# Turning the adjacency by VectorE and DRAM instead of by TensorE in the first graph stage

## The chip, the cores and the metric

The kernel runs on one core of one Trainium2 chip. The metric is the device time of one execution in microseconds (us); the number compared is the median over runs. The engines are named as the profile names them: PE is TensorE's matmul and PEld its weight load, DVE is VectorE, ACT is ScalarE, POOL is GpSimd and SP is SyncE. SPq and POOLq mark copies (DMAs) that SP and Pool put into their queues.

## The reference

There are 16 batches of 1024 nodes with 256 channels, and one adjacency `adj` of 1024 x 1024, all float32. Two layers follow each other:

```python
# layer 0: graph attention
h = relu(layernorm(x))
c = mean over channels of h                      # one value for each node
A = abs(abs(sigmoid(c_j - c_i) - 0.5) - 0.5) * 2
g = relu((h^T @ (adj * (A + A^T) / 2)) * para)   # becomes the queries
k, v = split(h @ kv_w)                           # 4 heads of 64
x = x + softmax(q k^T * scale) v
# layer 1: normalized adjacency and two linear layers
h = relu(layernorm(x))
A1 = adj + I
deg = colsum(A1) + rowsum(A1) - diag(A1)
A_hat = A1 * rsqrt(deg)[:, None] * rsqrt(deg)[None, :]
x = x + batchnorm(relu(batchnorm((A_hat @ h) @ W1^T + b1)) @ W2^T + b2)
```

Layer 0 needs `adj` as it lies in memory, weighted anew for each batch. Layer 1 needs `A_hat` transposed in SBUF (tile `f_ahatT`), because the contraction has to lie on the partitions. `f_ahatT` is made once, in the first batch's stages, and is used for the first time after the second batch's graph stage.

## The kernel before

The program is one instruction stream for each engine, in the order in which the code is written (`tc.manual_schedule`): no scheduler moves anything, and waits are by semaphores on the tiles. An engine that waits holds up everything that is queued behind the waiting instruction. SP and Pool issue copies in the same way, and each copy of a queue also waits for the landing of the one eight places before it in that queue.

For each batch b the stages are `graph(b)`, `attention(b)` and, one batch behind, layer 1's `linear1_all`. Batch 0 is prepared by a prologue. The partition count is P = 128, there are NC = 8 chunks of 128 nodes, and CC = 2 halves of the channels.

**Prologue.** SP loads x of batch 0, the eight adjacency tiles `f_adj`, `f_kvw`, x of batch 1 and `f_w1n`. The layer norm leaves `f_h_a` and the sums `f_sums`. `prepare_row(0)` turns the sums into rows with 16 small transposes on TensorE (L317 into `first`, L323 into `second`), VectorE copies `second` into `f_row` (L333), ScalarE makes the first weights `f_w` and VectorE masks them with `adj` (L336).

**graph(0).** For each chunk c a list of hooks runs, and then TensorE multiplies `f_h_a` with the weights `f_w` of chunk c into two PSUM tiles `f_gps` (L489, eight matmuls of 512 columns a chunk, four in each of the two halves' tiles). `weights(0, c)` is two ScalarE operations (L350, L353) and one VectorE mask (L367). `turn_h` transposes h in blocks (f_hQ, L378) and distributes the blocks by 16 copies on SP and 16 on Pool into `f_hT` (L385). At c = 5 SP issues the loads of `f_para` (L482). After the chunks VectorE multiplies `f_gps` with `f_para` into `f_qT` (L518), and the keys K and values V are made from `f_hT` by seven products each (class `Seven`; L428 and L433 on TensorE, L443 copies on ScalarE, L446 additions on VectorE). Their PSUM tiles come from a pool of three (`fps_s`, tag "s"), two of which `f_gps` holds until L518 has read them; `K.product(1)` takes the first that L518 frees, at 50.14 us.

**The turn of the adjacency.** Spread over the prologue and the hooks of chunks 1 to 5, `turn_adj(i)` and `turn_adj_aside(i)` transpose tile i in eight TensorE instructions (L1372; L1387 in two PSUM banks of other pools) and `place_adj` copies the result from PSUM to `f_ahatT` (L1378, L1393; seven tiles by VectorE, one by ScalarE). The view `columns(i)` orders the columns so that nodes of one residue modulo 8 stand together.

**After graph(0).** `diagonal()` runs on Pool: for each of eight blocks it multiplies the block with the identity into a spare tile (L1412) and adds the identity to it (L1413); VectorE reduces the products to `f_diag` (L1414). `column_sums(m)` are ScalarE copies with a running sum (L1404), two at the end of each of attention(0)'s four quarters; `roots` makes `f_dinv` from the sums after the last, and `scale_adj` applies it in graph(1) (L1433). Attention's quarters are 32 matmuls of scores (`f_s`, L868), ScalarE's exponentials (`f_p`, L876), VectorE's additions (L882, L888, L891, L896) and 32 matmuls with the values (`f_o`, L920). In the third quarter VectorE also inverts the softmax sums (`f_rec`, L953 and on) and ScalarE spreads them (`f_recs`, L962) ahead of the next quarter's exponentials.

Three small loads and stores come up in the prediction besides: `fw1T` and `fw2T` are the turned weights of the two linear layers on their way to DRAM (L1455, on Pool), `f_w2n` is the load of W2 in four copies of 32 partitions each (L1442, on SP), and `fw1s` and `f_att` are later copies on SP (L1158, L988).

Of the kernel before, what the change touches and what calls it, by code (L numbers as in the profile page):

```python
# [10 lines left out]
F32 = mybir.dt.float32  # L11
AF = mybir.ActivationFunctionType
ALU = mybir.AluOpType
AX = mybir.AxisListType
# [15 lines left out]
def fast_path(  # L30
# [37 lines left out]
    gs_d = [dram.tile([P, 4 * NC // 2, P], F32, tag=f"fgs_{b}", name=f"fgs_{b}") for b in range(B)]  # L68
    w1T_d = dram.tile([P, CC, F1], F32, tag="fw1T", name="fw1T")
    w2T_d = dram.tile([P, FC, C], F32, tag="fw2T", name="fw2T")  # L70
    w1s_d = dram.tile([P, 4, FC * P // 2], F32, tag="fw1s", name="fw1s")
    kvs_d = dram.tile([P, 8, P], F32, tag="fkvs", name="fkvs")
    t_d = [dram.tile([P, 4, 512], F32, tag=f"ft_{k}", name=f"ft_{k}") for k in range(3)]
# [104 lines left out]
    with ExitStack() as stage:  # L178
# [212 lines left out]
        class Seven:  # L391
# [50 lines left out]
            def copy(self, i, j):  # L442
                nc.scalar.copy(self.c(i, j), self.ps["x"])  # L443
# [26 lines left out]
        def graph(b, between):  # L470
# [42 lines left out]
            if b == 0:  # L513
                V, K = projections(b, kT, v, part, kt, key_sums[0])
                V.product(1)
                V.copy(0, 0)
                for d in range(CC):
                    nc.vector.tensor_mul(qT[:, d, :], gps[d], para_t[d])  # L518
                V.product(2)
                V.add(0, 0, 2)  # L520
                K.product(1)
                K.copy(0, 0)
                V.product(6)
                V.copy(1, 0)
                V.product(7)
                K.product(2)
                K.add(0, 0, 2)
                V.product(5)
                V.copy(1, 1)
                V.add(1, 0, 7)  # L530
                V.add(1, 1, 7)
                K.product(6)
                K.copy(1, 0)
                V.product(4)
                V.add(1, 0, 4)
                V.product(3)
                V.copy(0, 1)
                K.product(5)
                K.copy(1, 1)
                K.product(7)  # L540
                K.add(1, 0, 7)
                K.add(1, 1, 7)
                K.product(4)
                K.add(1, 0, 4)
                for d in range(CC):
                    nc.scalar.activation(qT[:, d, :], qT[:, d, :], AF.Relu, scale=-SCALE)
                K.product(3)
                K.copy(0, 1)
                return qT, kT, v
# [806 lines left out]
        def columns(i):  # L1356

            view = ahatT.rearrange("p m (i q) -> p m i q", i=NC)
            return view[:, :, :, ROW * i : ROW * (i + 1)]
# [6 lines left out]
        dinv = small.tile([P, NC], F32, tag="dinv", name="f_dinv", bufs=1)  # L1366
        drow = []

        def turn_adj(i):
            ps = ps_s.tile([P, NC, P], F32, tag="s", name=f"f_adjps_{i}")  # L1370
            for m in range(NC):
                nc.tensor.transpose(ps[:, m, :], adj_t[i][:, ts(m, P)], ident)  # L1372
            turned_adj[i] = ps

        turned_adj = {}

        def place_adj(i, copy):
            copy(columns(i), turned_adj.pop(i).rearrange("p m (q i) -> p m i q", i=NC))  # L1378

        def turn_adj_aside(i):  # L1380

            turned_adj[i] = [
                ps_o.tile([P, NC // 2, P], F32, tag="o", name=f"f_adjpsa_{i}"),
                ps_t.tile([P, NC // 2, P], F32, tag="t", name=f"f_adjpsb_{i}"),
            ]
            for m in range(NC):
                nc.tensor.transpose(  # L1387
                    turned_adj[i][m // 4][:, m % 4, :], adj_t[i][:, ts(m, P)], ident
                )

        def place_adj_aside(i, copy):
            for n, ps in enumerate(turned_adj.pop(i)):
                copy(columns(i)[:, 4 * n : 4 * n + 4], ps.rearrange("p m (q i) -> p m i q", i=NC))  # L1393

        def unused(name):
            return pp.tile([P, N], F32, tag="p", name=f"f_unused_{name}")
# [11 lines left out]
        def diagonal():  # L1408
            on = unused("d").rearrange("p (m q) -> p m q", q=P)
            for m in range(NC):  # L1410
                block = columns(m)[:, m]
                nc.gpsimd.tensor_mul(as_columns(on[:, m, :]), block, as_columns(ident))  # L1412
                nc.gpsimd.tensor_add(block, block, as_columns(ident))  # L1413
            nc.vector.tensor_reduce(diag, on, AX.X, ALU.add)  # L1414

        def roots():
            nc.vector.tensor_add(deg, rsum, deg)
# [41 lines left out]
        with tc.manual_schedule(engines={ENG.PE, ENG.Activation, ENG.DVE, ENG.Pool, ENG.SP}):  # L1459
# [13 lines left out]
            norm.relu(HALF, BY_VECTOR, False)  # L1473
            norm.vector_scale(BY_VECTOR, NC)
            hs[0] = norm.h
            turn_adj(0)
            place_adj(0, nc.vector.tensor_copy)
            xs[1] = load_x(1)
            prepare_row(0)
            turn_adj(1)  # L1480
            turn_adj_aside(2)
            place_adj(1, nc.vector.tensor_copy)
            weights(0, 1)

            w1n = load_rows(W1, FC, "w1")
# [2 lines left out]
            def load_w1T():  # L1488
# [3 lines left out]
                0,  # L1492
                {
                    0: [lambda: weights(0, 2), lambda: turn_h(0)],
                    1: [
                        lambda: place_adj_aside(2, nc.vector.tensor_copy),
                        lambda: weights(0, 3),
                        lambda: turn_adj(3),
                        lambda: place_adj(3, nc.scalar.copy),
                    ],  # L1500
                    2: [
                        lambda: weights(0, 4),
                        lambda: turn_weights(w1n, unused("w1Q"), w1T_d, FC),
                        lambda: prepare_start(1),
                        lambda: turn_adj_aside(4),
                        lambda: place_adj_aside(4, nc.vector.tensor_copy),
                    ],
                    3: [
                        lambda: weights(0, 5),
                        lambda: turn_adj(5),  # L1510
                        lambda: place_adj(5, nc.vector.tensor_copy),
                    ],
                    4: [
                        lambda: weights(0, 6),
                        lambda: weights(0, 7),
                        lambda: turn_adj_aside(6),
                        lambda: place_adj_aside(6, nc.vector.tensor_copy),
                        *(lambda m=m: row_sums(m) for m in range(NC)),
                    ],
                    5: [  # L1520
                        lambda: turn_adj(7),
                        lambda: place_adj(7, nc.vector.tensor_copy),
                    ],
                    6: [
                        lambda: prepare_end(1),
                        make_key_sums,
                        load_w1T,
                        lambda: again(0),
                    ],
                    8: [lambda: prepare_row(1)],  # L1530
                },
            )
            w2n = load_rows(W2, CC, "w2")
            w2Q, w1s_t = (w4.tile([P, N], F32, tag="w4", name=f"f_{n}") for n in ("w2Q", "w1s"))
            diagonal()
            for b in range(B):

                hooks, aside, behind = {}, {}, None
                if b + 1 < B:
# [8 lines left out]
                        behind = lambda: masked(b + 1, 1)  # L1548
                    if b == 0:
                        for m in range(NC):  # L1550
                            hooks.setdefault(m // 2, []).append(lambda m=m: column_sums(m))
                        hooks[1].append(lambda: turn_weights(w2n, w2Q, w2T_d, CC))
                        hooks[2].append(make_w1_sums)
                        hooks[3].append(roots)
# [978 lines left out]
```

## Time and profile before

| what | value |
|---|---|
| median of 3 runs | 2361.14 us (2360.05 to 2361.91) |
| profiled execution, its own time | 2359.81 us |
| its span in the profile | 2358.0 us |
| busy: PE, DVE, ACT, POOL | 2318.3, 1994.6, 1416.5, 447.6 us |
| first matmul of the first graph stage (L489) | 15.86 us |
| its last chunk over, first product for K and V (L433) | 48.35 us |
| first scores of attention(0) (L868) | 60.71 us |
| first chunk of graph(1) (L489) | 117.05 us |

Times within the execution are microseconds from the start of the span. A line of the timeline has the start, the length, the engine, the line of the code, the operation, output and input tiles, the shape and the number of instructions that were merged into the line; a bracket tells how long the engine sat idle before it and what ended that. The profile comes from one execution, so its durations are added up against that execution's own time.

### The profile page before, as it was taken

To read this page: it belongs to the slowest core of one execution; us is meant where nothing else is said; L and a number is where in the kernel's file an instruction comes from. 1 tells how busy PE (TensorE), PEld (TensorE's weight loads), DVE (VectorE), ACT (ScalarE), POOL (GpSimd) and SP (SyncE) were. 2 spreads that over 40 slices of the span, in tenths; PEclk is the share of its full clock that TensorE was granted. 3 is DMA by queue.
4 is the path that set the end of the run, shared out by engine and by line. 5 is a ranking of instruction groups with operands and counts; after the bars stand their busy time and mean duration, and the time that the engine had idled before them with its cause. 6 is when DMAs were issued, how large, how long until landed. Compare 5 with 4: busy or idle time off the path is not lost.

```text
span 2358.0 us, 25776 instructions
## 1 busy us (share of the span) xinstructions
PE 2318.3 (98%) x8256; PEld 1029.6 (44%) x8256; DVE 1994.6 (85%) x2937; ACT 1416.5 (60%) x2057; POOL 447.6 (19%) x573
## 2 busy tenths in 40 slices
PE   8999999999999999999999999999999999999995
PEld 5353444434343434444343434343444434444444
DVE  7988989898979899897989798988989898757766
ACT  6846556574838465655657384746556575346644
POOL 5121212122221112221212221221212121100000
PEclk9999999999999999999999999999999999999998
DMA  6143443423342434335343324252343421355569
GB/s 205 46 143 99 140 137 117 161 107 120 135 137 69 173 91 165 112 134 143 113 134 137 116 88 155 88 179 99 134 143 116 155 77 54 130 214 175 170 241 382
DMA packets 169217, 326.42 MB, mean 138 GB/s; under 512 B 34928, under 2 KB 102000, under 8 KB 169072
## 3 DMA queue, kind: packets, MB, share of 16 engines
q1 hardware_dynamic: 145264, 268.02, 33.3%
q0 software_dynamic: 19200, 39.88, 6.3%
q10 hardware_dynamic: 4608, 16.78, 1.8%
q8 instruction: 67, 1.10, 0.2%
q14 instruction: 78, 0.64, 0.1%
HBM read 203.96 MB, written 101.77 MB: 130 GB/s over the span
## 4 chain that ended last, share of the span: by engine, by line
PE 96%; DMA 1%; DVE 1%; ACT 1%; issue 0%; SPq 0%; DVEq 0%; ACTq 0%; POOLq 0%; POOL 0%
PE f_s L868 19%; PE f_o L920 19%; PE f_aps L1085 16%; PE f_gps L686 8%; PE f_zps L1195 7%; PE f_gpsx L686 6%; PE f_zx L1755 4%; PE f_zm L1755 3%; PE f_vpsx L433 2%; PE f_kpsx L428 2%; PE f_gps L489 2%; PE f_vps L433 2%; PE f_kps L428 2%; PE f_outps L1973 1%; PE f_zps L1278 1%; PE f_zps3b L1195 1%
## 5 line engine op out<-in xcount | busy, mean ns | idle before, releaser
L876 ACT ACTIVATE f_p<-f_s 128x1024 f32<-128x1024 f32 x512 | 476.9, 1045 | 59.5 <-PE f_s L868 59.5
L868 PE MATMUL f_s<-f_qT,f_kT 64*128 64x512 f32 x2048 | 456.8, 596 | 0.0
L920 PE MATMUL f_o<-f_p,f_v 128*64 128x512 f32 x2048 | 453.6, 595 | 0.0
L868 PEld LDWEIGHTS f_s<-f_qT,f_kT 64*128 64x128 f32 x2048 | 191.2, 185 | 263.7 <-issue 118.0
L920 PEld LDWEIGHTS f_o<-f_p,f_v 128*64 128x64 f32 x2048 | 141.4, 137 | 304.3 <-issue 264.2
L363 POOL TENSOR_TENSOR f_w<-f_w,f_adj 128x1024 f32<-128x1024 f32 x56 | 132.2, 2361 | 701.3 <-ACT f_w L362 528.7
L988 POOL DMA_DIRECT2D f_att<-f_oT x256 | 136.1, 539 | 342.9 <-DVE f_oT L971 337.3
L891 DVE TENSOR_TENSOR f_acc<-f_acc,f_p 128x1024 f32<-128x1024 f32 x128 | 155.9, 1218 | 4.6 <-ACT f_p L876 4.6
L891 DVE TENSOR_TENSOR f_sums<-f_sums,f_p 128x1024 f32<-128x1024 f32 x128 | 155.8, 1218 | 0.0
L350 ACT ACTIVATE f_w<-f_row,f_col 128x1024 f32<-128x1024 f32 x127 | 147.4, 1160 | 13.8 <-DMA f_row<-frow 11.5
L353 ACT ACTIVATE f_w<-f_w 128x1024 f32<-128x1024 f32 x127 | 134.3, 1058 | 4.0
L1085 PE MATMUL f_aps<-f_ahatT,f_hs 128*128 128x512 f32 x256 | 115.1, 592 | 0.0
L1085 PE MATMUL f_aps<-f_ahatT,f_h_b 128*128 128x512 f32 x256 | 112.6, 592 | 0.0
L1085 PE MATMUL f_aps<-f_t,f_hs 128*128 128x512 f32 x256 | 112.5, 592 | 0.0
L362 ACT ACTIVATE f_w<-f_w,f_now 128x1024 f32<-128x1024 f32 x56 | 64.3, 1149 | 76.0 <-DVE f_now L360 76.0
L686 PE MATMUL f_gps<-f_w,f_h_a 128*128 128x512 f32 x224 | 109.8, 592 | 0.0
L882 DVE TENSOR_TENSOR f_acc<-f_p,f_p 128x1024 f32<-128x1024 f32 x64 | 77.9, 1217 | 25.0 <-ACT f_p L876 25.0
L888 DVE TENSOR_TENSOR f_sums<-f_p,f_p 128x1024 f32<-128x1024 f32 x64 | 78.1, 1221 | 20.2 <-ACT f_p L876 20.1
L367 DVE SCALAR_TENSOR_TENSOR f_w<-f_w,f_adj 128x1024 f32<-128x1024 f32 x71 | 87.9, 1257 | 7.8 <-ACT f_w L353 7.7
L283 ACT ACTIVATE f_h_a<-f_x,f_shift_a,f_rstd_a 128x256 f32<-128x256 f32 x126 | 73.8, 587 | 31.9 <-DVE f_shift_a L268 31.8
L1218 ACT ACTIVATE f_z<-f_zps,f_b 128x512 f32<-128x512 f32 x60 | 38.0, 684 | 75.2 <-PE f_zps L1195 75.2
L283 ACT ACTIVATE f_h_b<-f_x,f_shift_b,f_rstd_b 128x256 f32<-128x256 f32 x128 | 66.2, 592 | 25.8 <-DVE f_shift_b L268 25.8
(297 smaller groups left out, 3981.9 us busy)
## 6 DMA issues: line engine op xcount, KB each, us to landing
f_t<-ft SPq DMA_DIRECT2D x84, 512.0 KB, 9.7
fz<-f_z SPq DMA_DIRECT2D x64, 512.0 KB, 9.7
f_x<-in_x_dram SPq DMA_DIRECT2D x31, 1024.0 KB, 6.1
f_zb<-fz SPq DMA_DIRECT2D x42, 512.0 KB, 4.5
fx<-f_x SPq DMA_DIRECT2D x16, 1024.0 KB, 4.4
fgs<-f_gs POOLq DMA_DIRECT2D x28, 512.0 KB, 3.0
fhT<-f_hQ POOLq DMA_DIRECT2D x112, 128.0 KB, 3.2
f_hT<-fhT SPq DMA_DIRECT2D x28, 512.0 KB, 6.4
```

Source lines behind the costliest of these rows:

```text
L283: nc.scalar.activation(self.h[:, c, :], self.xt[:, c, :], AF.Relu, bias=self.shift[:, c : c + 1], scale=self.rstd[:, c : c + 1], accum_out ...
L350: nc.scalar.activation(w, rows[b], AF.Abs, bias=cols[b][:, c : c + 1], scale=0.5 / C)
L353: nc.scalar.activation(w, w, AF.Tanh)
L686: nc.tensor.matmul(ps, left, right, start=fresh and n == 0, stop=(n == PAIRS - 1), skip_group_check=more,)
L868: nc.tensor.matmul(ps[:, e, :], kT[rows_e, pair, ts(m, P)], qT[rows_e, pair, ts(g, 512)], start=True, stop=True,)
L876: nc.scalar.activation(p, ps, AF.Exp)
L891: nc.vector.tensor_add(to, to, p)
L920: nc.tensor.matmul(o_of[s][e * HD : (e + 1) * HD, :], v[:, m, ts(2 * pair + e, HD)], p[:, e, :], start=(m == 0), stop=(m == NC - 1),)
L988: queue.dma_start(t[ts(j, 32), :, a].rearrange("r h c i -> r h (c i)"), oT[ts(a, 32), :, j].rearrange("r h c i -> r h (c i)"),)
L1085: nc.tensor.matmul(ps, left[:, m, :], right(m), start=not more and m == 0, stop=(m == KH - 1), skip_group_check=more,)
L1195: nc.tensor.matmul(ps[i], left[:, ts(i, P)], right, start=not more, stop=True, skip_group_check=more,)
L1755: nc.tensor.matmul(ps, left[:, m, :], right[:, m, :], start=start and m == 0, stop=(m == 1), skip_group_check=not start,)
```

## The change

The turn of `adj` leaves TensorE. The adjacency is loaded a second time with its rows in another order (`by_rows`: node number 8u + i, so that 32 partitions hold rows u of one residue i), VectorE transposes it in blocks of 32 x 32 into `f_ahatT`, which serves as a staging area (`stage_rows`), Pool stores the blocks to a DRAM tile `fadjT` so that they land where the transposed matrix wants them, and SP loads the whole of it back into `f_ahatT`. Each of these copies is written for 32 partitions at a time; the stores go in runs of 128 elements. Half of the rows is loaded before the first graph stage (on Pool's queue, into the still unused tiles `kT` and `qT`), the other half on SP behind the `f_hT` copies. Four turns run in the hooks of chunks 1 to 3, four among the K and V products ("first" and "then"); `prepare_row(1)` moves to "first". VectorE's reduction for the diagonal moves from the place before attention(0) to the end of the third quarter, and the column sums from two in every quarter to none, two, three and three.

```diff
+    adjT_d = dram.tile([N, N], F32, tag="fadjT", name="fadjT")
...
                 V.add(0, 0, 2)
+                for step in between["first"]:
+                    step()
                 K.product(1)
...
                 V.add(1, 1, 7)
+                for step in between["then"]:
+                    step()
                 K.product(6)
...
-        def turn_adj(i):
-            ps = ps_s.tile([P, NC, P], F32, tag="s", name=f"f_adjps_{i}")
-            for m in range(NC):
-                nc.tensor.transpose(ps[:, m, :], adj_t[i][:, ts(m, P)], ident)
-            turned_adj[i] = ps
...
+        stage_rows = ahatT.rearrange("p m x -> p (m x)").rearrange("p (k t r) -> p k t r", k=32, t=NC)
+        by_rows = adj.rearrange("(u i) d -> i u d", i=NC)
+        adj_rows = {}
+        def load_adj(t0, home, n, queue):
+            pool, tag, bufs = home
+            t = pool.tile([P, n, N], F32, tag=tag, name=f"f_adjr_{t0}", bufs=bufs)
+            first = 32 * (t0 % 4)
+            for a in range(4):
+                queue.dma_start(
+                    t[ts(a, 32)],
+                    by_rows[2 * a + t0 // 4, first : first + 32 * n].rearrange(
+                        "(e r) d -> r e d", e=n
+                    ),
                 )
+            for e in range(n):
+                adj_rows[t0 + e] = t[:, e]
+        def load_adj_early():
+            for t0, tag in ((0, "kT"), (2, "qT")):
+                load_adj(t0, (big, tag, 1), 2, nc.gpsimd)
+        def load_adj_late():
+            for t0, home in enumerate(
+                ((ow, "oT", 2), (ow, "oT", 2), (ow, "att", 1), (pp, "p", NC)), 4
+            ):
+                load_adj(t0, home, 1, nc.sync)
+        def turn_adj(t):
+            nc.vector.transpose(
+                stage_rows[:, :, t], adj_rows.pop(t).rearrange("p (k s) -> p k s", s=32)
+            )
+        def store_adj(half):
+            to = adjT_d.rearrange("(k s) (a g x) -> g a s k x", s=32, a=4, g=2)[half]
+            for a in range(4):
+                nc.gpsimd.dma_start(
+                    to[a],
+                    stage_rows[ts(a, 32), :, 4 * half : 4 * half + 4].rearrange(
+                        "p k t r -> p k (t r)"
+                    ),
+                )
+        def reload_adj():
+            whole = adjT_d.rearrange("(m p) x -> p m x", p=P)
+            for m in range(0, NC, 2):
+                nc.sync.dma_start(ahatT[:, m : m + 2], whole[:, m : m + 2])
...
-            nc.vector.tensor_reduce(diag, on, AX.X, ALU.add)
+            return lambda: nc.vector.tensor_reduce(diag, on, AX.X, ALU.add)
...
-            turn_adj(0)
-            place_adj(0, nc.vector.tensor_copy)
             xs[1] = load_x(1)
+            load_adj_early()
             prepare_row(0)
-            turn_adj(1)
-            turn_adj_aside(2)
-            place_adj(1, nc.vector.tensor_copy)
...
+                    1: [lambda: turn_adj(0), lambda: weights(0, 3)],
                     2: [
                         lambda: weights(0, 4),
+                        lambda: turn_adj(1),
+                        load_adj_late,
+                        lambda: weights(0, 5),
                         lambda: turn_weights(w1n, unused("w1Q"), w1T_d, FC),
                         lambda: prepare_start(1),
...
                     3: [
+                        lambda: weights(0, 6),
+                        lambda: turn_adj(2),
+                        lambda: turn_adj(3),
+                        lambda: store_adj(0),
+                        lambda: weights(0, 7),
                     ],
...
+                    4: [lambda m=m: row_sums(m) for m in range(NC)],
...
-                    8: [lambda: prepare_row(1)],
+                    "first": [lambda: turn_adj(4), lambda: turn_adj(5), lambda: prepare_row(1)],
+                    "then": [lambda: turn_adj(6), lambda: turn_adj(7), lambda: store_adj(1)],
...
-            diagonal()
+            reload_adj()
+            sum_diagonal = diagonal()
...
-                            hooks.setdefault(m // 2, []).append(lambda m=m: column_sums(m))
+                            hooks.setdefault((m + 4) // 3, []).append(lambda m=m: column_sums(m))
+                        hooks[2].append(sum_diagonal)
```

## The prediction

> **What bounds the kernel now.** I read the page first: TensorE is busy 98% of the span and the chain that ended last is 96% TensorE. A stage can give back only the TensorE time that is taken out of it, and every wait put in front of TensorE is paid in full.
>
> ```profile
> PE 2318.3 (98%) x8256; PEld 1029.6 (44%) x8256; DVE 1994.6 (85%) x2937; ACT 1416.5 (60%) x2057; POOL 447.6 (19%) x573
> ...
> PE 96%; DMA 1%; DVE 1%; ACT 1%; issue 0%; SPq 0%; DVEq 0%; ACTq 0%; POOLq 0%; POOL 0%
> ```
>
> Then the timeline of TensorE over the first 130 us (start, length, line, tiles, count):
>
> ```profile
> 9.55 1.94 PE L1372 MATMUL f_adjps<-f_ident,f_adj 128*128 128x128 f32 x8 [9.55 <-DMA f_adj<-in_adj_dram]
> ...
> 12.81 1.04 PE L323 MATMUL f_rps<-f_ident,f_sums 128*128 128x128 f32 x8
> 13.69 1.04 PE L1372 MATMUL f_adjps<-f_ident,f_adj 128*128 128x128 f32 x8
> ...
> 15.86 3.67 PE L489 MATMUL f_gps<-f_w,f_h_a 128*128 128x512 f32 x8 [0.26 <-DVE f_w L336]
> 19.37 1.04 PE L1372 MATMUL f_adjps<-f_ident,f_adj 128*128 128x128 f32 x8
> ...
> 38.05 10.47 PE L489 MATMUL f_gps<-f_w,f_h_a 128*128 128x512 f32 x24
> 48.35 1.05 PE L433 MATMUL f_vpsx<-f_kvw,f_hT 128*128 128x128 f32 x8
> ...
> 50.14 1.02 PE L428 MATMUL f_kpsx<-f_hT,f_kvw 128*128 128x512 f32 x2
> ```
>
> From 9.55 us on there is hardly a gap, so the turns of the adjacency cost TensorE time from 15.86 on; the three groups before that fill a wait for the first weights. The same eight turns take 1.94 us at 9.55 and 1.04 us at 13.69: TensorE starts at half rate. Next the SP queue's timeline, VectorE's, and bytes by window (columns: stretch, length, busy times, clock, DMA share, GB/s):
>
> ```profile
> 22.30 11.53 SPq L385 DMA_DIRECT2D f_hT<-f_hQ  x16
> 33.94 3.79 SPq L482 DMA_DIRECT2D f_para<-in_L_gnn_para_dram  x2
> ```
>
> ```profile
> 26.75 1.24 DVE L1449 STREAM_TRANSPOSE f_unused_w1Q<-f_w1n 128x1024 f32<-128x1024 f32 x1
> ...
> 42.79 1.01 DVE L455 TENSOR_TENSOR f_kt<-f_hT,f_hT 128x512 f32<-128x512 f32 x1
> ...
> 46.89 1.21 DVE L518 TENSOR_TENSOR f_qT<-f_gps,f_para 128x1024 f32<-128x1024 f32 x1
> ...
> 50.41 0.69 DVE L446 TENSOR_TENSOR f_v<-f_v,f_vps 128x512 f32<-128x512 f32 x1 [0.63 <-PE f_vps L433]
> ```
>
> ```profile
> 12.00:18.00 6.00, 5.74 (x35) 4.41 (x34) 4.65 (x7) 4.89 (x7) 0.00 (x0) 1.00 1.03 411
> 62.00:63.00 1.00, 1.00 (x8) 0.39 (x4) 0.18 (x1) 1.00 (x2) 0.00 (x0) 1.00 0.91 209
> ```
>
> f_para is issued the moment f_hT is out; the product with it at 46.89 frees the PSUM tile that K.product(1) (50.14) needs. Copies over 128 partitions move 411 GB/s; the copies of f_w2n to 32 partitions each (62 to 63) move 209 with the engines 91% busy.
>
> **TensorE turns removed.** Eight groups; the three before 15.86 lie in a wait. The other five cost 0.87 us each from start to start (13.69 to 14.56), with a wait of 0.2 before one: 4.6 us. The whole stage agrees: eight chunks without turns between them are 27.5 (the last three take 48.35 - 38.05 = 10.3, so 3.44 each), against 48.35 - 15.86 = 32.5 now. So 5.0 us is the most that can be won; nothing else on TensorE is taken out.
>
> **The warm start is lost.** The removed turns at 9.55 are what brings TensorE to full rate at about 12.6. After the change its first work is the 16 single transposes of L317 and L323, which follow f_sums, and then a wait until f_w at about 16.3 (L323 at half rate ends 0.45 later, and L333 and L336 queue behind it on VectorE). Bounds for running L489 at half rate: nothing, or 3.1 us (9.55 to 12.6) of it, costing 1.5. Work this sparse is nearest to the idle start, so 1.5. TensorE would end the chunks at 16.3 + 1.5 + 27.5 = 45.3 instead of 48.35. The Trainium skill, TensorE: Matmul & The Clock Gate, Part 1, says that half clock is the default, released after about 3.4 us of activity and restored after an idle window. By that page alone the start would cost an estimated 1.7 us.
>
> **VectorE and ScalarE in this stage.** Out: four copies of 1.22 (L1378) and six of 0.68 (L1393), 9.0 us, and one ScalarE copy, 0.99. In: eight stream transposes of 1.24 (row L1449), 9.9 us, four in the chunks, four in the projections. They queue ahead of f_w3, f_w5 and f_w7; laid end to end by the rows after the two f_hQ transposes (they end at 23.4), f_w3 is ready at 25.8, f_w6 at 35.0, f_w7 at 38.5, and TensorE, at 3.44 us a chunk, asks for them at 28.1, 38.4 and 41.9. This hides the sum if the adjacency rows land in time. The early 2.1 MB (2 x 1.05) are issued by Pool, which is free from 10.2, and share the 411 GB/s with SP's loads: the first 1.05 MB at half of it take 5.1 us, and with about 1 us to start and 2.6 to land (row fw1s) they are there near 19, wanted at 23.4. But they push all that SP has queued back by 2.1 / 0.411 = 5.1 us. f_w1n, issued last at 17.9 with a landing of 8.6, goes from 26.5 to 31.6, wanted at 29.2: VectorE waits 2.4, within the 3.4 that f_w6 and f_w7 have. The f_hT copies follow, as each SP copy waits for the landing of the eighth before it: they are out at 34 to 39 instead of 33.8, and I take 36, as only those behind f_w1n wait.
>
> **The late rows stand in front of f_para.** load_adj_late puts 16 copies on SP between f_hT and f_para. Lower bound: 0.44 us of issue each (row f_w1n), 7.0, and f_para's median landing of 4.3, all hidden from other traffic and after f_hT at 34: f_para lands at 45.3. Upper bound: 2.1 MB to 32 partitions each at 209 GB/s are 10.0 us; store_adj(0) sends another 2.1 MB by Pool from 37.4 (VectorE ends the fourth turn), nearest row again 209, 10.0 us, all of it ahead; then 1.3 for f_para's bytes and 2.6 to land: 36 + 10 + 10 + 3.9 = 60. The two queues interleave, so neither end is likely: 53. L518 then starts at 53 instead of 46.89, K.product(1) at 54.6 instead of 50.14: **+4.5 us**. TensorE has run V.product(1) and (2) and stands from 47.1 to 54.6. Going on after such a pause is bounded by nothing and the 1.5 of half rate; nearest is the slow start after 9.55 us of idling: **+1.4**. VectorE's transposes in "first" and "then" (5.0 us) stand before the additions L446, where it has 2.8 and 2.0 us of idling before the last ones; attention's first PSUM tile needs V's addition 4 at about 10.7 after f_para, TensorE comes there 10.6 after K.product(1): nothing.
>
> **The way back and the diagonal.** store_adj(1) starts at about 63; 10 to 14 us later SP's reload_adj (4.2 MB at 411, 10.2 us) fills ahatT in quarters from about 82 to 91. Behind it on SP queue only fw1s and f_att; neither is due before 101. Pool's sixteen small operations follow each quarter and end near 94; fw2T behind them is not read before 1977. ScalarE's first column sums are wanted at 85 plus the delay, 92: covered by some 7 us; without cover ScalarE's next f_p wait, and TensorE, microsecond for microsecond. But Pool now runs beside attention, where VectorE idles 0.85 us in the third quarter (0.56 before L888, 0.29 before L891). The row: L455 takes 1.01 beside Pool and its like 0.69 (L446); f_kt's four additions take 3.9 instead of 2.8, f_kvs's eight 3.6 instead of 2.2 (0.28 each when alone): 2.5 us lost in 7.0 beside Pool. In the new place two thirds of VectorE's 11 us beside Pool are such additions: about 2.7. With f_diag's reduction (L1414, 1.21) moved into the same quarter: 2.7 + 1.2 - 0.85 = 3.0 late at f_rec, of which ScalarE's wait of 0.78 and a spare PSUM tile of 0.4 take 1.3: **+1.7** (0 to 3). The Trainium skill, SBUF — State Buffer, Who interferes with whom, calls the port that VectorE and GpSimd share an exclusive lock, the loser blocking for the whole instruction. By it the sixteen operations of 0.52 could hold VectorE up for an estimated 8.3 us; the rows show a partial loss. The third column sum in quarters three and four (1.13 each) lies under ScalarE's waits of 1.67 and 3.12.
>
> **Sum.** 4.5 + 1.4 + 1.7 = 7.6 us later. On the profiled execution (span 2358.0, its own time 2359.81) that is 2367.4; the median 2361.14 is 1.3 above it, so 2368.7.
>
> **The rivals.** *Everything lands in time*: f_para by 45.3, Pool harmless. Then K.product(1) follows the chunks, 2.9 earlier than before: 2358.2; with no half rate either 2356.2, the floor. For it: the windows 40 to 44 show the queues at 62 GB/s, room for the late rows. Against: store_adj(0) falls into that room. It decides as soon as f_para lands before 48.8 (50.14 less 1.3). *Fabric fully serial*: f_para at 60, +11.5, and 1.5 and 3: 2377. *The change does its part and both ends cancel*: f_para at 49 to 50, Pool's loss about 1: 2361 to 2365.
>
> **How the numbers follow.** About 0.2% (4.7 us) is what a measurement tells from no change. Slower by more, f_para after about 50.3 with the other two terms: 0.62 (own range 2366 to 2376). Within: 0.33, the cancelling case and most of the in-time one. Faster by more needs the floor with nothing lost: 0.05. Range 2358 to 2376.
>
> **What would show it** (lines of the changed kernel). Right: a wait of TensorE before L429 (f_kpsx) ended by VectorE's product with f_para, that product waiting for its load near 53, slow matmuls at 16, additions over 1.22 us while Pool multiplies the diagonal. Wrong: L519 following gps without a wait, or ScalarE's column sums waiting for the reload, a cost that I put at nothing.

## The result and the profile after

The changed kernel takes 2384.51 us (median of five runs, 2382.99 to 2385.25) against 2361.14 before: a ratio of 1.0097, 95% interval 1.0085 to 1.0108. Slower was right; the size was not: 2368.7 was forecast, and 2384.5 lies above the range, which ended at 2376. The profiled span is 2382.7 us against 2358.0, so 24.7 us have to be found. Lines of the changed kernel are one to five higher than before in the first graph stage and in attention (L489 is L490, L428 is L429, L482 is L483, L518 is L519, L868 is L873); the load and the turn of `f_w1n` move from L1442 and L1449 to L1471 and L1478. TensorE's timeline after (start, length, line, tiles, count, idle time and what ended it):

```profile
16.49 22.79 PE L490 MATMUL f_gps<-f_w,f_h_a 128*128 128x512 f32 x48 [1.92 <-DVE f_w L337]
44.20 8.83 PE L490 MATMUL f_gps<-f_w,f_h_a 128*128 128x512 f32 x16 [4.92 <-DVE f_w L368]
52.86 1.05 PE L434 MATMUL f_vpsx<-f_kvw,f_hT 128*128 128x128 f32 x8
...
70.56 2.08 PE L429 MATMUL f_kpsx<-f_hT,f_kvw 128*128 128x512 f32 x2 [15.75 <-DVE f_qT L519]
```

The last line stood at 50.14 before. First scores start at 83.45 instead of 60.71 (22.7 later) and graph(1) at 141.26 instead of 117.05 (24.2 later); behind it the two kernels run alike within 0.5 us. The queues and VectorE tell where the 22.7 us come from. SP's queue:

```profile
12.99 16.26 SPq L1471 DMA_DIRECT2D f_w1n<-in_L_gnn_W_dram  x4
29.36 16.11 SPq L386 DMA_DIRECT2D f_hT<-f_hQ  x16
45.51 17.02 SPq L1384 DMA_DIRECT2D f_adjr<-in_adj_dram  x16
62.63 0.83 SPq L483 DMA_DIRECT2D f_para<-in_L_gnn_para_dram  x2
```

VectorE's two waits, each for one of these copies:

```profile
38.39 1.25 DVE L1478 STREAM_TRANSPOSE f_unused_w1Q<-f_w1n 128x1024 f32<-128x1024 f32 x1 [8.47 <-DMA f_w1n<-in_L_gnn_W_dram]
...
69.28 2.52 DVE L519 TENSOR_TENSOR f_qT<-f_gps,f_para 128x1024 f32<-128x1024 f32 x2 [17.19 <-DMA f_para<-in_L_gnn_para_dram]
```

Each step starts where the one above ended: f_w1n takes 16.3 us of the queue (5.5 before), f_hT 16.1 (11.5 before), and f_para goes out at 62.6 instead of 33.9. The windows (length, busy times of PE, PEld, DVE, ACT and POOL, clock, DMA share, GB/s) show why:

```profile
12.00:14.00 2.00, 2.00 (x10) 2.00 (x11) 0.13 (x1) 1.06 (x2) 2.00 (x5) 1.00 1.02 408
16.00:28.00 12.00, 11.51 (x23) 5.12 (x24) 9.60 (x10) 10.57 (x10) 2.73 (x6) 1.00 1.04 265
...
68.00:70.00 2.00, 0.00 (x0) 0.00 (x0) 0.72 (x1) 0.00 (x0) 0.00 (x0) 0.50 1.00 408
```

The DMA engines are full in all three, but from 16 to 28, when the early rows are under way, they move 265 GB/s instead of 408. The last line also shows TensorE's granted clock at 0.50 in its pause.

### The profile page after: what moved, and what is told of

The parts are those of the page before. It is cut to its first block, busy times and chain, and to the rows that moved or that the text cites. A ratio compares the mean times of both kernels' runs of the same rounds, so it can differ in the third digit from the quotient of the medians.

```text
span 2382.7 us, 25712 instructions
## 1 busy us (share of the span) xinstructions
PE 2321.7 (97%) x8192; PEld 1027.3 (43%) x8192; DVE 1995.2 (84%) x2935; ACT 1415.6 (59%) x2056; POOL 463.0 (19%) x589
## 4 chain that ended last, share of the span: by engine, by line
PE 94%; DMA 2%; SPq 1%; DVE 1%; ACT 0%; issue 0%; POOL 0%; DVEq 0%; ACTq 0%; POOLq 0%
PE f_s L873 19%; PE f_o L925 19%; PE f_aps L1090 16%; PE f_gps L691 8%; PE f_zps L1200 6%; PE f_gpsx L691 6%; PE f_zx L1771 4%; PE f_zm L1771 3%; PE f_vpsx L434 2%; PE f_kpsx L429 2%; PE f_kps L429 2%; PE f_vps L434 2%; DMA f_x<-in_x_dram 1%; PE f_gps L490 1%; PE f_outps L1989 1%; SPq L1384 1%
## 5 line engine op out<-in xcount | busy, mean ns | idle before, releaser
L873 PE MATMUL f_s<-f_qT,f_kT 64*128 64x512 f32 x2048 | 457.3, 596 | 1.0 <-ACT f_p L881 1.0
L873 PEld LDWEIGHTS f_s<-f_qT,f_kT 64*128 64x128 f32 x2048 | 190.9, 185 | 265.5 <-ACT f_p L881 117.1
L351 ACT ACTIVATE f_w<-f_row,f_col 128x1024 f32<-128x1024 f32 x127 | 147.2, 1159 | 15.7 <-DMA f_row<-frow 10.3
```

What stands on the lines that cost most here:

```text
L351: nc.scalar.activation(w, rows[b], AF.Abs, bias=cols[b][:, c : c + 1], scale=0.5 / C)
L873: nc.tensor.matmul(ps[:, e, :], kT[rows_e, pair, ts(m, P)], qT[rows_e, pair, ts(g, 512)], start=True, stop=True,)
```

## The experiments

The first matmul of L490 starts between 15.7 and 17.2 us by when the inputs happen to land, so a difference of 1 us between first scores of two runs is nothing, and e8, which turned out to repeat e2, lies 2.1 us from it. "Attention" is the time from the first scores to graph(1). Rows are called narrow when each copy goes to 32 partitions, and wide when it goes over all 128; the way back is `reload_adj`.

| kernel | median us | first scores | attention | span |
|---|---|---|---|---|
| before | 2361.14 | 60.71 | 56.34 | 2358.0 |
| the change | 2384.51 | 83.45 | 57.81 | 2382.7 |
| e1, no late rows | 2374.14 | 65.59 | 64.40 | 2371.4 |
| e2, no early rows | 2371.29 | 71.36 | 57.69 | 2371.6 |
| e3, no rows | 2367.21 | 57.88 | 63.75 | 2363.7 |
| e4, f_para first | 2382.67 | 68.12 | 71.93 | 2381.3 |
| e8, e2 with stores in "then" | 2370.05 | 69.27 | 57.71 | 2368.7 |
| e9, e1 with wide rows | 2368.20 | 59.51 | 64.95 | 2365.4 |
| e10, e2 with wide rows | 2367.45 | 59.65 | 65.63 | 2365.5 |
| e11, e2, store(0) last | 2364.79 | 58.62 | 62.53 | 2362.2 |
| f2, both wide | 2370.69 | 69.25 | 57.69 | 2368.9 |
| e12, no rows, no ways | 2357.49 | 58.61 | 56.68 | 2356.2 |
| e5, e3 with row back | 2366.45 | 60.16 | 63.07 | 2365.9 |
| e6, e5 with warm-up | 2364.95 | 58.32 | 64.35 | 2363.2 |
| e7, e5 without diagonal | 2363.09 | 60.09 | 60.05 | 2361.5 |
| f1, reordered | 2373.95 | 63.31 | 65.31 | 2371.7 |
| f3, f1 with warm-up | 2372.48 | 63.47 | 67.74 | 2372.6 |

### Which half of the rows costs what: e1, e2, e3

```diff
-                        load_adj_late,                # e1 and e3
+                        lambda: adj_rows.update({t: adj_t[t] for t in range(4, NC)}),
-            load_adj_early()                          # e2 and e3
+            adj_rows.update({t: adj_t[t] for t in range(4)})
```

> The late half of the rows is not loaded; the turns 4 to 7 read the adjacency as it lies in SBUF instead, so that half of the transposed matrix is not the reference's. Early loads, turns, stores and the way back stay. Theory (two separate delays: the early rows slow SP's loads down, the late rows stand in front of f_para): the early damage stays, VectorE waits about 8.5 us for f_w1n and TensorE 4.9 us for f_w; f_hT is out at 45.5, f_para is issued there instead of at 62.6 and lands, beside store_adj(0), near 52, so K.product(1) starts near 54 instead of 70.6, and the span falls by 15 to 17 us, to 2366 to 2368. Rival (the store and the blocks' traffic hold f_para up whoever issues what first): f_para still lands after 60 and the span stays above 2375.

> The early half of the rows is not loaded; the turns 0 to 3 read the adjacency as it lies in SBUF instead, so that half of the transposed matrix is not the reference's. The late loads stay in front of f_para. Theory (two separate delays): f_w1n lands near 26.5 as before, no wait of 8.5 us on VectorE and none of 4.9 us on TensorE; f_hT is out near 34, the 16 late copies take about 17 us of SP's queue beside store_adj(0), f_para is issued near 51 and lands near 57, K.product(1) starts near 58.5; the span is about 2370 to 2372. Rival (the late copies were slow only because the early loads had delayed everything into the store): with the fabric free at 34 they take 7 to 10 us, f_para lands by 49 and the span is 2362 to 2364.

> Neither half of the rows is loaded; all eight turns read the adjacency as it lies in SBUF, so that the transposed matrix is not the reference's. Turns, stores, way back, column sums and diagonal stay as in the changed kernel. Theory (the row loads are what costs): f_hT is out at 34, f_para is issued there and lands before 45, TensorE ends the chunks near 45.5 after a start at half rate, K.product(1) follows near 47.5; with about 1.5 us lost beside Pool in attention the span is 2356 to 2359, not slower than before. Rival (slow clock, stores, turns and the diagonal are half of the loss): span above 2366.

Against e3, the early half alone puts the first scores 7.7 us later (e1), the late half alone 13.5 (e2), both together 25.6: 4.4 more than the sum. The expected chains are there. In e1 VectorE waits 8.70 us for f_w1n and TensorE 4.85 for f_w, and f_para, issued at 45.1, has landed when VectorE asks for it at 52.3. In e2 both those waits are gone and K.product(1) starts at 58.27 (58.5 expected), though by other parts: the late copies took 11.7 us of SP (17 expected), f_para then 11.9 to land.

What no theory had is in e1's and e3's last columns. In e3 the first graph stage is 2.8 us shorter than before, as the rival *everything lands in time* had it (2.9), and yet the kernel is slower than before (1.0027, 1.0014 to 1.0040), because attention takes 7.4 us longer. ScalarE's timeline in e3 names the wait, SP's the chain behind it:

```profile
73.84 1.15 ACT L351 ACTIVATE f_w<-f_row,f_col 128x1024 f32<-128x1024 f32 x1 [6.75 <-DMA f_row<-frow]
```

```profile
47.60 3.02 SPq L313 DMA_DIRECT2D frow<-f_sums  x1
64.08 0.33 SPq L314 DMA_DIRECT2D f_row<-frow  x1
```

The sums of batch 1 go to DRAM (4 KB in pieces of 4 bytes) and come back as f_row. Before, the store went out at 45.9, took 13.7 us to land and the load 6.2: f_row was there at 65.9 and wanted at 69.2. Here it is wanted at 67.1, 2.1 us sooner, while the store is issued 3.0 us instead of 0.6 and lands after 16.4, the load after 9.7. TensorE loses 4.2 us in the second quarter, behind this wait, and 3.0 in the fourth, where it waits for ScalarE again; e7 below shows that the diagonal has a part in the latter. In the change as it stands nobody sees f_row's lateness, since the wait for f_para gives it all the time it needs (there at 86.4, wanted at 92.6).

### Only the order on SP: e4

```diff
-                        load_adj_late,                # hook of chunk 2
+                        load_adj_late,                # hook of chunk 6, behind f_para
```

> Nothing is left out. The 16 late copies are issued after the two f_para loads (in the hook of chunk 6, behind chunk 5's f_para) instead of before them. Theory: f_para is issued at 45.5 and lands near 52, L519 no longer waits until 69; but the late rows now land between 52 and 68 and the turns 4 and 5 stand on VectorE before the additions of the products, so VectorE waits for f_adjr and TensorE for PSUM tiles: about half of the 16 us come back, span 2372 to 2376. Rival (the wait only moves from f_para to f_adjr): span within 2 us of 2382.7.

The rival's number (within 2 us of 2382.7) for neither's reason. First scores come 15.3 us earlier; VectorE waits 4.38 us for f_adjr, far less than feared. But frow now stands behind the late copies on SP, goes out at 65.2 and takes 20.8 us to land, and attention pays 15.6 us:

```profile
91.00 1.15 ACT L351 ACTIVATE f_w<-f_row,f_col 128x1024 f32<-128x1024 f32 x1 [13.41 <-DMA f_row<-frow]
```

### Bytes or form: e9, e10, f2; the store: e8, e11

```diff
-            for a in range(4):                        # rows of f_adjr, 32 partitions a copy
-                queue.dma_start(t[ts(a, 32)], by_rows[...])
+            for e in range(n):                        # e9: early, e10: late, f2: both
+                queue.dma_start(t[:, e], adj[ts(t0 + e, P)])
```

> As e1_no_late_rows, with the early 2.1 MB loaded by four copies over all 128 partitions (4 KB to each) instead of eight over 32 partitions each; the rows then come in their plain order, so that the transposed matrix is not the reference's. Bytes, queue and place stay. Theory (the form of the copies makes the fabric slow: 260 GB/s instead of 411): f_w1n lands near 31 instead of 38, VectorE waits for it under 3 us instead of 8.7, TensorE not at all for f_w (4.9 in e1), f_hT is out by 39, first scores at 58.5 to 61 instead of 65.6. Rival (it is the bytes ahead of f_w1n, whatever their form): VectorE still waits over 6 us for f_w1n and the first scores come after 64.

> As e2_no_early_rows, with the late 2.1 MB loaded by four copies over all 128 partitions instead of sixteen over 32 each, in front of f_para as there; plain order of rows, so that the transposed matrix is not the reference's. Theory (the form and number of the late copies): four issues of 0.45 us instead of 11.7 us of SP's queue, f_para is issued by 36 and lands near 44, L519 waits for it under 1 us, K.product(1) at 48 to 50 instead of 56 to 58. Rival (bytes beside store_adj(0)): f_para still lands after 50 and TensorE waits over 4 us before K.product(1).

The theory holds in e9. In e10 it holds for TensorE, but f_para lands at 46.4 and not near 44, and VectorE waits 4.7 us for it, not under 1. The same 2.1 MB go to the same place, spread over 128 partitions: in e9 VectorE waits 1.82 us for f_w1n, TensorE does not wait, f_hT is out at 38.4. The windows of e1 and then of e9 over the same 12 us:

```profile
16.00:28.00 12.00, 11.48 (x22) 5.08 (x23) 9.56 (x10) 10.53 (x10) 2.50 (x5) 1.00 1.03 255
```

```profile
16.00:28.00 12.00, 11.23 (x20) 4.97 (x21) 10.00 (x11) 9.90 (x10) 3.65 (x8) 1.00 1.05 379
```

Both are full; one moves half as much again. In the trace the median 4 KB packet takes about 260 ns in e1 and 164 ns in e9 (both from 16 to 23 us). In e10 the late rows leave SP in 2.07 us instead of 11.67, and K.product(1) follows without a wait at 48.46. Both then wait for f_row in attention (8.22 and 7.02 us).

These runs change three things at once: the spread over partitions, the number of copies (four instead of eight or sixteen) and the order of the rows in DRAM (neighbours instead of every eighth). The order alone does not make a packet slow: in the change, with the narrow rows' order, the median 4 KB packet of the late rows took 159 ns between 46 and 62. The number of copies was not separated from the spread; "form" below means the two together.

The Trainium skill, SBUF — State Buffer, Door 1: The DMA port swizzle, says that 32 neighbouring partitions reach 8 of the 16 ports, about 218 GB/s, and 128 reach all. The runs agree in direction: 255 GB/s with narrow rows on two queues at once, 379 to 411 wide; e11 below moves 260 with the late rows alone, more than the page's figure for one copy. It is the page that spoke against this change, and the forecast did not weigh it.

```diff
-                        lambda: store_adj(0),         # hook of chunk 3
+ "then": [..., lambda: store_adj(0), lambda: store_adj(1)],   # e8
+ "then": [..., lambda: store_adj(1), lambda: store_adj(0)],   # e11
```

> As e2_no_early_rows (the first four turns read the adjacency as it lies, the late rows are loaded in front of f_para), and store_adj(0) is issued with store_adj(1) after the projections' turns instead of in the hook of chunk 3. Theory (it is the store beside them that makes the late rows and f_para slow): the 16 late copies leave SP in 8 to 9 us instead of 11.7, f_para lands by 48, K.product(1) starts at 48 to 51 instead of 58.3. Rival (32-partition copies are slow by themselves): K.product(1) still starts after 55. The span is no measure here, as the way back and f_row come later.

> As e2_no_early_rows, with store_adj(0) issued behind store_adj(1) on Pool, so that it waits for the last turn; in e8 it had not moved, since Pool has nothing else to do before it. Theory (the store beside them slows the late rows and f_para): the late copies leave SP in 8 to 9 us instead of 11.7 to 13.3, f_para lands by 48, K.product(1) at 48 to 51 instead of 56 to 58. Rival (the late copies are slow by themselves): K.product(1) still after 54.

e8 tested nothing: Pool had no work before the store, so that it went out at 37.69 as ever (first scores 69.27: a repeat of e2, 2.1 us from it). An engine's order is its own; writing a step later moves it only past that engine's other steps. In e11 the store waits for the last turn, and the theory holds:

```profile
32.31 9.24 SPq L1384 DMA_DIRECT2D f_adjr<-in_adj_dram  x16
41.65 0.83 SPq L483 DMA_DIRECT2D f_para<-in_L_gnn_para_dram  x2
```

K.product(1) is at 47.97 without a wait. So, here, narrow rows beside no store are fast enough, and so are wide rows beside the store; narrow rows beside a narrow store are not. But the way back is now late, and what the forecast had put at nothing is seen in ScalarE's column sums (TensorE then waits 2.97 us in the third quarter; f_row was waited for too, 4.96 us):

```profile
89.51 1.06 ACT L1433 ACTIVATE f_ahatT<-f_ahatT 128x1024 f32<-128x1024 f32 x1 [4.52 <-POOL f_ahatT L1442]
```

> The whole change with queues, places and order as they are, but both halves of the rows loaded over 128 partitions (four copies each, 4 KB to each partition), in their plain order, so that the transposed matrix is not the reference's. Theory (the form of the copies is what makes the first stage 22.7 us longer): f_hT is out near 38.5, f_para is issued by 43 and lands near 50, first scores at 61 to 64 instead of 83.5; f_row then keeps attention(0) waiting as in e9 and e10, span 2367 to 2371. Rival (4.2 MB of rows and 2.1 MB of store are too much for the fabric in any form): f_para lands after 58, first scores after 70.

First scores at 69.25 lie between theory and rival: form alone takes back 14.2 of the 22.7 us, the chunks run without a wait, but f_para, issued at 41.4, still lands after 13 to 15 us, behind 2.1 MB of rows and beside the narrow store (TensorE waits 8.24 us before K.product(1)). What is left is bytes and no longer a slow rate, for the engines now move 392 GB/s, the store included:

```profile
46.00:56.00 10.00, 1.76 (x17) 1.57 (x15) 1.23 (x1) 1.91 (x7) 0.00 (x0) 0.75 1.03 392
```

The span fits the expectation by another route, for f_row was in time.

### What is left of the change without its traffic: e12, e5, e6, e7

e12 is e3 without store_adj and reload_adj. e5 is e3 with prepare_row(1) back in hook 8. e6 adds three groups of eight unread transposes to e5, e7 takes the diagonal out of it.

```diff
+            warm(1)                                   # e6: 8 transposes of f_adj at 9.5 us
...
             prepare_row(0)
+            warm(2)                                   # e6: 16 more
-                nc.gpsimd.tensor_mul(as_columns(on[:, m, :]), block, as_columns(ident))   # e7
-                nc.gpsimd.tensor_add(block, block, as_columns(ident))                     # e7
```

> As e3_no_rows, with the two stores to DRAM and the way back left out as well: of the change only the turns on VectorE, the diagonal's new place and prepare_row(1) in "first" are left, the transposed matrix is not the reference's. Theory (in e3 it is the stores beside it that make the store and load of f_row late): frow is issued in under 1 us instead of 3, f_row lands by 68 instead of 74, ScalarE waits for it under 1.5 us instead of 6.75, attention(0) takes 56.5 to 58.5 us instead of 63.8 and the span is 2355 to 2358, faster than before by the 2.8 us of the first stage at most. Rival (f_row was late because the stage before it is shorter and it starts from ScalarE's work, not from the queue): ScalarE still waits over 4 us, span above 2360.

Theory. In attention, which takes 56.68 us, neither ScalarE waits for f_row nor TensorE for anything, and the kernel is faster than before: 0.9983 (0.9973 to 0.9992). SP's chain in the quiet:

```profile
48.33 0.57 SPq L313 DMA_DIRECT2D frow<-f_sums  x1
61.39 0.33 SPq L314 DMA_DIRECT2D f_row<-frow  x1
```

f_row lands at 67.2 and ScalarE takes it up at 67.7: 3.3 us of slack before, 0.5 now. The store starts 2.5 us later than before even here, so the rival has a part in it, but it is the traffic of the stores and the way back, taken out together here, that makes e3's 6.75 us.

> As e3_no_rows (no second load of the rows, the turns read the adjacency as it lies in SBUF), and prepare_row(1) is put back in front of the projections (hook 8), where it stands in the kernel before. Theory: in e3 the first graph stage was 2.8 us shorter than before, but ScalarE waited 6.75 us in the first quarter of attention for f_row, whose store frow goes out on SP only after the two turns of "first" and takes some 16 us to land; with prepare_row(1) early again f_row is there by about 67, that wait falls below 2 us, attention(0) takes 57.5 to 58.5 us instead of 63.8, and the span is 2357 to 2359. Rival (column sums, Pool's diagonal and the reduction make up the loss in attention): the wait for f_row goes but attention(0) still takes over 61 us, span above 2361.

A miss. frow is issued no earlier (48.5), because it waits for ScalarE's sums and not for VectorE; f_row is waited for as long (6.32 us). And prepare_row(1) in hook 8 makes VectorE wait for those sums ahead of L519, which costs TensorE 1.14 us.

> As e5_row_back, and TensorE does three groups of eight transposes whose result nobody reads, one at 9.5 us and two behind the transposes of f_sums. Theory (the lost warm start costs 1.5 us): the first matmuls of L490 run at full rate, the chunks end near 44 instead of 45.4, first scores near 56.4 instead of 57.9, span 1 to 1.5 below that of e5. Rival (VectorE sets the end of the projections, not TensorE): the chunks end earlier but TensorE then waits for it before the scores, and the span is that of e5 within 0.5 us.

```profile
16.66 29.83 PE L490 MATMUL f_gps<-f_w,f_h_a 128*128 128x512 f32 x64 [1.92 <-DVE f_w L337]
```

```profile
16.91 27.73 PE L490 MATMUL f_gps<-f_w,f_h_a 128*128 128x512 f32 x64 [0.17 <-DVE f_w L337]
```

The first line is e5, the second e6: warm, the 64 matmuls take 2.1 us less, and the first scores come 1.8 earlier. Attention gives 1.3 of it back, 1.0 of that to the wait for f_row (7.31 instead of 6.32), so that graph(1) starts only 0.6 earlier. The medians are 1.5 apart as expected, but their intervals against before overlap.

> As e5_row_back, with the diagonal left out: Pool's sixteen operations beside attention and VectorE's reduction are gone, f_diag is set to zero. Theory (my term of 1.7 us for Pool beside VectorE and the reduction): VectorE's additions in the second quarter take 1.22 us instead of 1.53, attention(0) takes 56.3 to 56.8 us as before, span 1 to 1.7 below that of e5. Rival (the losses lie under waits of other engines): VectorE's additions are shorter, the span is the same within 0.5 us.

Theory, with more than its number: attention is 3.0 us shorter. At 60.05 it is still far from the 56.3 to 56.8 expected, since the wait for f_row stays (7.21). One of VectorE's additions in the second quarter of e5 and of e7:

```profile
84.52 1.54 DVE L893 TENSOR_TENSOR f_sums<-f_p,f_p 128x1024 f32<-128x1024 f32 x1
```

```profile
84.79 1.22 DVE L893 TENSOR_TENSOR f_sums<-f_p,f_p 128x1024 f32<-128x1024 f32 x1
```

### The whole change in another order: f1, f3

```diff
             w1n = load_rows(W1, FC, "w1")
+            load_adj_early()                          # on SP, behind f_w1n
...
                         lambda: weights(0, 7),
+                        lambda: turn_adj(3),
+                        load_adj_late,                # on Pool, behind its f_hT copies
...
-                            hooks.setdefault((m + 4) // 3, []).append(lambda m=m: column_sums(m))
+                            hooks.setdefault((m + 8) // 4, []).append(lambda m=m: column_sums(m))
```

> The whole change with nothing left out, in another order: the early rows go out on SP behind f_w1n instead of on Pool ahead of it, the late rows on Pool behind the f_hT copies instead of on SP in front of f_para, the turns 0 to 3 come one to two chunks later, both stores stand behind the last turn, and the column sums move to the ends of the third and fourth quarter (four each). Theory (all of the 22 us in the first stage come from what the 32-partition copies stand in front of and beside): VectorE waits under 2 us for f_w1n and TensorE not at all for f_w, f_para lands before 48, first scores at 58.5 to 61, attention(0) takes 58 to 60 us, span 2359 to 2363: as before. Rival (the rows, stores and f_hT copies share one fabric and order does not matter): first scores after 66, span over 2368.

> As f1_reordered, with the three groups of eight unread transposes of e6 in front of the first matmuls. Theory: the chunks end 1.5 to 2 us earlier than in f1 as in e6; with f_para in time the first scores come 1.5 to 2 us earlier, but f_row, whose way through DRAM starts from ScalarE's work, does not, so that half of it is lost to ScalarE's wait: span 0.5 to 1.5 below that of f1. Rival (VectorE's turns, now later, set the end of the projections): span as f1.

f1 is 10.6 us faster than the change and still slower than before (1.0058, 1.0042 to 1.0075), between theory and rival in the first stage; its span of 2371.7 is where the rival had it, over 2368. VectorE waits 4.72 us for the early rows, f_hT is out at 41.7, the late rows are waited for up to 2.16 us, frow takes 20.5 us from issue to the load behind it:

```profile
51.72 0.57 SPq L313 DMA_DIRECT2D frow<-f_sums  x1
72.19 0.33 SPq L314 DMA_DIRECT2D f_row<-frow  x1
```

f3 starts warm and finds only more to wait for (1.93 us for f_w, 3.44 for f_para): first scores as f1. Its median is 1.5 lower; the two intervals overlap. No run with its data intact beat the kernel before, and e12, which leaves all of the change's traffic out, gains 3.6 us; e12 with a warm start was not run.

## Why the prediction was right and wrong

By the steps of its sum: 4.5 + 1.4 + 1.7 = 7.6 was forecast, 20.4 + 2.3 + 1.5 = 24.2 measured, the rest of the 24.7 lies behind graph(1).

**The late rows in front of f_para** (4.5 forecast, 20.4 measured) is the term that failed: the place was right, the size was not. It had two mis-sized parts, 9.5 us and 6.7 us.
- *f_hT out at 36* (45.5 measured). I let the early rows share 411 GB/s, the rate of copies over 128 partitions, though they are copies to 32, for which the next line of my own fence gave 209. At 265 GB/s f_w1n's turn came at 38.4, not 31.6. e9, with wide copies, gave nearly the forecast's own numbers: turn at 32.0, a wait of 1.8 (2.4 forecast), f_hT out at 38.4 (34 to 39 forecast).
- *f_para at 53* (69.2 measured). The bounds of 45.3 and 60 were counted from f_hT out at 34 and at 36. From f_hT out, f_para took 23.7 us, against 23.9 for my upper, serial end (10 + 10 + 3.9). I took a value between the ends because the queues interleave; but the engines were full, and served two narrow queues no faster than one: 232 GB/s for rows and store in the change, 260 for the late rows alone in e11. The rival *fabric fully serial* was the right mechanism, with its 36 too early.

```profile
46.00:64.00 18.00, 8.81 (x31) 4.71 (x29) 5.99 (x15) 5.37 (x17) 3.16 (x4) 0.78 0.93 232
```

```profile
34.00:42.00 8.00, 8.00 (x20) 3.53 (x19) 7.89 (x16) 8.00 (x15) 2.46 (x1) 1.00 0.96 260
```

That the rate was mis-sized, and not the place, is seen in f2: with both halves wide the product with f_para comes at 54.6 (53 forecast) and K.product(1) at 55.9 (54.6 forecast).

The 209 itself was right by luck. From 62 to 63 the trace has 49 packets of 4 KB, which are f_row's load to all partitions, and 4 of 2 KB, which are f_w2n's. Mostly f_w2n's packets (98 against 2) move from 64 to 65, and that row reads 209 as well:

```profile
64.00:65.00 1.00, 1.00 (x6) 0.47 (x6) 1.00 (x1) 1.00 (x2) 0.00 (x0) 1.00 1.03 209
```

**VectorE's wait for f_w1n, costed at nothing.** 2.4 us against a slack of 3.4 was forecast; it was 8.47, and TensorE waited 4.92 and then ran the last chunks slowly (8.83 us instead of 6.9). All of that disappeared under the wait for f_para, which e1 shows by taking that one away: first scores still 4.9 us later than before.

**TensorE turns removed, start at half rate.** 16.3 for the start was 16.5; the gain of 5.0 is there where nothing holds it up (e3 ends its chunks at 45.44, forecast 45.3). Half rate cost 2.1 by e6, not 1.5. After the pause it cost 2.3 (12.9 us from K.product(1) to the scores, 10.6 before), forecast 1.4: the granted clock reads 0.50 from 58 to 74.

**VectorE's transposes, column sums, way back: nothing.** Right in the change (the column sums start without a wait at 108.79), but covered by its own lateness. e11 shows a wait of 4.5 us on ScalarE, and 2.97 on TensorE, when the cover is gone.

**Pool beside VectorE, the reduction.** 1.7 forecast, 1.5 for all of attention in the change, 3.0 in e5 against e7, where f_row's wait had already used up attention's slack. The additions took 1.53 us beside Pool instead of 1.22: a partial loss, as the rows of before said. Each of them lost 0.3 us beside one Pool operation of 0.52, so the estimate from the Trainium skill, SBUF — State Buffer, Who interferes with whom, was too high; the page says of such additions, with both inputs in SBUF, that they contend with GpSimd's reads, and gives the block for a whole instruction for VectorE's two-port modes.

**Not in the forecast: f_row.** prepare_row(1)'s store and load were a step that the change moves, and I gave them no line. In the change they cost nothing; but beside the stores they, and the diagonal's part in attention, keep the rival *everything lands in time* (2358.2) out of reach: e3 realised its first stage and came to 2367, while e12, without stores and way back, came to 2357.5.

## What to carry to other kernels

Price a new copy by the rate of rows of its own form, and price what stands behind it in its queue by that same rate: a full DMA share says nothing of GB/s (here 1.04 at 265 and 1.02 at 408). When a bound's upper end is "all of it in series" and the engines are already full, take series seriously: here it was the case. Before a stage is shortened, list every chain that starts from something else and ends in the next stage (here sums to DRAM and back, with 3.3 us of slack): what a stage gains above that slack is handed to that chain.

## What the runs showed of the hardware

- Loads to 32 partitions slowed down the loads beside them: 255 to 265 GB/s at a share above 1.0, the median 4 KB packet about 260 ns instead of 164 on both queues (e1, e9). A store from 32 partitions beside wide loads did not: 392 GB/s in f2, 165 ns a packet.
- A store of 4 KB in pieces of 4 bytes takes 13.0 us to land in the quiet and up to 23.7 beside others (e1), and its issue 0.57 us or up to 9.6 (f2).
- The granted clock reads 1.00 in the windows from 16 to 22 of e5, in which the first matmuls run slowly (3 in the 2 us from 18, 5 in the next 2, then 6); after the pause in the change it reads 0.50, and two matmuls take 2.08 us instead of 1.02. So it showed only one of the two slow stretches.
